# Two graph attention layers on one core: where a tile's own row joins its early sum

## The chip, the cores and the metric

The kernel runs on one core of a Trainium2 chip. The metric is the device time of one execution in microseconds (us), as the median of several runs. Beside it stands one profiled execution, from which every duration below is taken.

## The reference

Two layers of graph attention over 3327 nodes with 1024 features, with an adjacency matrix of zeros and ones (about 16 neighbours per node, each node its own neighbour too). Cut to what matters:

```python
def layer0(x, adj, W, a_src, a_dst):             # 8 heads of 128
    h = (x @ W).reshape(C, H, D)
    e = leaky_relu(alpha_src[:, :, None] + alpha_dst[:, None, :], 0.2)
    e = where(adj == 0, -inf, e)
    return softmax(e) @ h                        # per head

x = layernorm(x + layer0(x, adj, W0, a_src, a_dst))
x = layernorm(x + relu(layer1(x, adj, W1, a1, a2)))   # the same with one head
```

A node's result is a weighted mean of its neighbours' rows of h. The node's own row is one of them, with a weight of its own: per head the larger of two products of exponentials, times the diagonal of the adjacency matrix.

## The kernel before

Nodes are handled in 26 tiles of 128. The kernel has three stages.

**Stage one, tables and lists (0 to 604 us).** For each tile PE multiplies its x with the weight matrix in three column groups (`project`, L554), ACT copies each group out of PSUM (`keep`), and SP stores the row of h with its score factors to a table in HBM, `h0_d`. Two PSUM banks alternate for these groups. `flip` transposes x tiles on PE and ACT copies them (L204). Beside this, three Python generators are advanced a step at a time from inside `project`, by `pace`, four times in a column group, 12 times in a tile; the instruction order of every engine is this order, written out by hand.

- `counting`: a row of the adjacency matrix (loaded with a cast to bytes by POOL's queue into one of three masks `ad`) is counted by ACT (`words`, L354) and packed by DVE.
- `listing`: for each tile DVE takes the neighbours out of the packed words (`keys`, `columns`, L313, L315), ACT and DVE compute the place of each row's neighbours in the tile's list (`ways`, `places`, `spread`), PE sorts them into the list (`give`, L474, L467), ACT copies the list out (`take`, L486 to L493) and DVE turns it into indices (`sources`, L501 to L515). Before that, `ends` (L370) and `ends2` (L394) compute where each row's part of the list begins and ends: a small multiply by PE with a triangle of ones, a copy by ACT (L375, L395), and about ten small operations on POOL, once a tile each. `mvs` and `place_of` are their buffers, four of each.
- `sums_so_far` (from tile 13 on): the neighbours that lie in the first half of the table can be summed for 17 "early" tiles while the second half is still being computed. For each tile and each of two blocks, POOL issues four indirect gathers of `h0_d` rows (`fetch`, L672) into one of three buffers (`near`, `near`, `far`), DVE makes the weights (`marks`, `weights`, L689 to L693), and PE multiplies (`sums`, L702) into one PSUM tile of three banks. The generator yields nine times per early tile, so that it is spread over nine slots. At the end of a tile ACT copies the three parts to `z` (L742) and SP stores them to `half_d`.

```python
for n in range(3):
    nc.scalar.activation(by_head(z)[...], acc[:, n, :nh, :], AF.Copy)
nc.sync.dma_start(half_d[s], z)
```

**Stage two, layer 0 (604 to about 1190 us).** One tile after the other, late and early ones mixed, the first one late. Late tiles gather four blocks and a rest (17 indirect gathers), early ones two blocks and a rest (9), into five buffers. `prepare` loads the tile's own row of the table (L1077) and, for early tiles, the stored sum (L1080). DVE computes the own weights from the own row (`own`, L1086 to L1088), ACT scales the row head by head (`scale_own`, L1095), and PE adds it, and for early tiles the stored sum, to the sums in PSUM by a multiply with the identity (L1126). The gathered blocks are weighted by DVE (L1113) and summed by PE (L1139, L1131). `finish` divides, normalises and stores the row to a second table.

**Stage three, layer 1 (to 1844 us).** The same with one head from the second table, with a dense multiply after it (L1271).

Of the kernel before, what the change touches and what calls it, by code (L numbers as in the profile page):

```python
# [26 lines left out]
def kernel(  # L27
# [67 lines left out]
    XS = 256  # L95
    chunks = [(c, min(CT, NT - c)) for c in range(0, NT, CT)]
# [41 lines left out]
    def by_head(row):  # L138
        return row[:, :DW].rearrange("p (h d) -> p h d", h=H)

# [36 lines left out]
    class Phase:  # L177
# [84 lines left out]
        def edge_constants(self):  # L262
# [29 lines left out]
            self.mvs = [self.pool.tile([P, 3, NY], BF16, bufs=1, name=f"mvs{n}") for n in range(4)]  # L292
            for mv in self.mvs:
                nc.vector.memset(mv, 0.0)
                nc.vector.tensor_scalar(mv[:, 0, XN : XN + 1], nums, 1.0, None, op0=OP.add)
                nc.vector.tensor_scalar(mv[:, 0, NY - 1 :], part[:, 0, NB - 1 :], 1.0, None, op0=OP.add)
# [21 lines left out]

    class Edges:
# [6 lines left out]
        def __init__(self, ph, t):  # L326
            self.ph, self.t = ph, t
            self.d, self.end2 = cnt[:, t, :2], cnt[:, t, 2:3]

        def factors(self):  # L330

            mv = self.ph.mvs[self.t % 4][:, :, XR:XL]
            r = self.ph.sbuf("r0", [P, 2, H], 2)
            nc.scalar.activation(r[:, 0, :], sd0[:, self.t, 0, :], AF.Exp, scale=1 - SLOPE)
            nc.gpsimd.tensor_copy(mv[:, 0, :], r[:, 0, :])
            nc.gpsimd.tensor_tensor(r[:, 1, :], r[:, 0, :], mv[:, 0, :], OP.subtract)
            nc.gpsimd.tensor_copy(mv[:, 1, :], r[:, 1, :])
            nc.gpsimd.tensor_tensor(mv[:, 2, :], r[:, 1, :], mv[:, 1, :], OP.subtract)
# [8 lines left out]
        def words(self, ad, junk):  # L347

            sbuf = self.ph.sbuf
            for n in range(2):
                nc.scalar.activation(junk, ad[:, n * THR : (n + 1) * THR], AF.Copy, accum_out=self.d[:, n : n + 1])  # L354
            self.deg_b = sbuf("deg_b", [P, 2], 16, dt=BF16)
            nc.scalar.activation(self.deg_b, self.d, AF.Copy)
            w = ad.bitcast(I32)
            for n in range(3):
                m = WD >> n
                half = w[:, :m] if n == 1 else sbuf(f"wd{n}", [P, m], 16 if n == 2 else 1, dt=I32)  # L360
                nc.vector.scalar_tensor_tensor(
                    half, w[:, m:], 1 << n, w[:, :m], op0=OP.logical_shift_left, op1=OP.bitwise_or
                )
                w = half
            self.bytes = w.bitcast(U8)

        def ends(self, tri_b):

            op = self.ph.dd[:, self.t % 4 * 4 : self.t % 4 * 4 + 2]
            nc.tensor.matmul(op, tri_b, self.deg_b, start=True, stop=True)  # L370
            v = self.ph.sbuf("place_of", [P, 20], 4)
            end, off, low = (v[:, n : n + 2] for n in (0, 2, 4))
            self.mid, self.over = v[:, 6:8], v[:, 8:10]
            self.more, self.mid2, self.start, self.off2 = (v[:, n : n + 1] for n in range(10, 14))
            nc.scalar.activation(end, op, AF.Copy)  # L375
            self.more_b = self.ph.sbuf("more_b", [P, 1], 4, dt=BF16)
            nc.gpsimd.tensor_tensor(off, end, self.d, OP.subtract)
            nc.gpsimd.tensor_tensor(self.mid, off, end, OP.add)
            nc.gpsimd.tensor_scalar(low, off, float(HG2), None, op0=OP.max)
            nc.gpsimd.tensor_scalar(end, end, float(HG2), None, op0=OP.max)  # L380
            nc.gpsimd.tensor_tensor(self.over, end, low, OP.subtract)
            nc.gpsimd.tensor_tensor(self.more, self.over[:, :1], self.over[:, 1:], OP.add)
            nc.gpsimd.tensor_copy(self.more_b, self.more)
            nc.gpsimd.tensor_scalar(
                off[:, :1], off[:, :1], self.d[:, 1:], self.over[:, :1], op0=OP.subtract, op1=OP.subtract
            )
            mv = self.ph.mvs[self.t % 4][:, :, : XB + 1 : XB]
            nc.gpsimd.tensor_copy(mv[:, 0, :], off)
            nc.gpsimd.tensor_tensor(mv[:, 1, :], off, mv[:, 0, :], OP.subtract)

        def ends2(self, all_b):

            op = self.ph.dd[:, self.t % 4 * 4 + 2 : self.t % 4 * 4 + 3]
            nc.tensor.matmul(op, all_b, self.more_b, start=True, stop=True)  # L394
            nc.scalar.activation(self.end2, op, AF.Copy)  # L395
            nc.gpsimd.tensor_tensor(self.start, self.end2, self.more, OP.subtract)
            nc.gpsimd.tensor_tensor(self.mid2, self.start, self.end2, OP.add)
            nc.gpsimd.tensor_scalar(
                self.off2, self.start, self.d[:, 1:], self.over[:, 1:], op0=OP.subtract, op1=OP.add
            )  # L400
            mv = self.ph.mvs[self.t % 4][:, :, XE : XE + 1]
            nc.gpsimd.tensor_copy(mv[:, 0, :], self.off2)
            nc.gpsimd.tensor_tensor(mv[:, 1, :], self.off2, mv[:, 0, :], OP.subtract)
# [35 lines left out]
        def places(self):  # L439

            sbuf, ph, pack, away = self.ph.sbuf, self.ph, self.pack, self.away
            mv = self.mv = ph.mvs[self.t % 4]
# [75 lines left out]
    with ExitStack() as own, tc.manual_schedule():  # L518
# [10 lines left out]
        lists = [Edges(ph, t) for t in range(NT)]  # L529
# [6 lines left out]
        def load_mask(t):  # L536
            if t < NT:
                ads[t] = masks[t % 3]
                if t == NT - 1:
                    nc.vector.memset(ads[t].bitcast(I32), 0)  # L540
                    nc.vector.memset(ads[t][:, :1], 1.0)
                for r in pieces(t):
                    nc.gpsimd.dma_start(ads[t][r, :N], adj[at(t, r), :])
# [59 lines left out]
        def listing():  # L603

            for t in range(-1, NT):
                old, new = lists[t] if t >= 0 else None, lists[t + 1] if t + 1 < NT else None
                for s in range(4):
# [4 lines left out]
                    if s == 1 and 2 < t + 3 < NT:  # L612
                        need(t + 3)
                        lists[t + 3].ends(tri_b)
                    if s == 3 and 2 < t + 3 < NT:
                        lists[t + 3].ends2(all_b)
# [40 lines left out]
        def sums_so_far():  # L657

            acc = part.bank("L", [P, 3, HALF], "part")
            acc = acc[:, :, : 3 * DH1].rearrange("p n (h d) -> p n h d", h=3)  # L660
# [37 lines left out]
            def sums(acc, val, b, e, heads_):  # L698
                vals = val[:, :, :DW].rearrange("p g (h d) -> p g h d", h=H)
                for h in heads_:  # L700
                    for g in range(NG):
                        nc.tensor.matmul(  # L702
                            acc[g * GT : (g + 1) * GT, h // 3, h % 3, :], e[:, g, h, :], vals[:, g, h, :],
# [7 lines left out]

            res = [listed(0), listed(1)]
            for _ in range(3):
                yield
            for n in range(2):
# [3 lines left out]
                yield  # L719
            oh = marks(0)  # L720
            fetch(2)
            yield
            yield
            for s in range(EARLY):
                for b in range(HB):
                    n = s * HB + b
                    val = src[n % 3]
                    e = weights(val, b, res[0], oh)
                    yield
                    if n:  # L730
                        fetch(n + 2)
                    yield
                    sums(acc, val, b, e, range(H // 2))
                    yield
                    sums(acc, val, b, e, range(H // 2, H))
                    if b == 0:
                        yield
                        yield
                z = part.sbuf("z", [P, DW], 1)
                for n in range(3):  # L740
                    nh = HEADS[n + 1] - HEADS[n]
                    nc.scalar.activation(by_head(z)[:, HEADS[n] : HEADS[n + 1], :], acc[:, n, :nh, :], AF.Copy)  # L742
                nc.sync.dma_start(half_d[s], z)
                if s + 2 < EARLY:
                    res.append(listed(s + 2))
                res.pop(0)
                if s + 1 < EARLY:
                    oh = marks(s + 1)
# [21 lines left out]
        masks = [pool.tile([P, NP], U8, bufs=1, name=f"ad{n}") for n in range(3)]  # L770
# [56 lines left out]
        part.more_banks(own, "part", {"L": 1})  # L827
# [12 lines left out]
        ph.edge_constants()  # L840

# [15 lines left out]
        lists[0].ends(tri_b)  # L857
# [5 lines left out]
        lists[0].ends2(all_b)  # L863
        flip(3, 0)
        load_x(5)
        lists[1].ends(tri_b)
# [5 lines left out]
        lists[1].ends2(all_b)  # L872
# [3 lines left out]
        lists[2].ends(tri_b)  # L876
        project(3, 0)
        keep(3, 0)
        lists[2].ends2(all_b)
        for t in range(3, NT):  # L880
# [3 lines left out]
            if t == 12:  # L884
# [11 lines left out]
            if t == 16:  # L896
# [80 lines left out]
    def sparse(own):  # L977
# [82 lines left out]
        class Layer0:  # L1060
# [10 lines left out]
            def prepare(self):  # L1071
# [5 lines left out]
                nc.sync.dma_start(self.h, h0_d[self.t * P : (self.t + 1) * P, :HW0])  # L1077
                if self.t < EARLY:
                    self.half = sbuf("xT", [P, DW], 2, "half")
                    nc.sync.dma_start(self.half, half_d[self.t])  # L1080

            def own(self):

                t, h = self.t, self.h
                es = self.es = sbuf("es0", [P, H], 2)
# [4 lines left out]
            def scale_own(self):  # L1090

                h = self.h
                for n in range(H):
# [25 lines left out]
            def sums(self, b):  # L1119
# [3 lines left out]
                for n in self.banks.get(j, ()):  # L1123
                    for row in (self.h, self.half) if self.t < EARLY else (self.h,):
                        part = row[:, HEADS[n] * DH1 : HEADS[n + 1] * DH1]
                        nc.tensor.matmul(  # L1126
                            self.acc[n].rearrange("p h d -> p (h d)"), ident, part, start=False, stop=False
                        )
# [415 lines left out]
```

## Time and profile before

| | |
|---|---|
| median of 3 runs | 1784.67 us (1782.95 to 1788.36) |
| profiled execution | 1845.9 us |
| its span, first to last instruction | 1844.2 us |
| PE / DVE / POOL / ACT busy over the span | 88% / 62% / 59% / 28% |
| moved by DMA | 594.27 MB, mean 322 GB/s |
| mean granted TensorE clock | 0.943 |

A line of a window table gives the stretch, its length, then for PE, PEld (weight loads), DVE, ACT and POOL the busy time and the number of instructions, then the granted clock, the DMA share (busy share of the 16 DMA engines) and the GB/s moved. A line of the waits gives who waited for whom, the total, the number of times and the longest. The profile ends PE instructions by a model, so that a busy PE need not be PE at its peak[...].

### The profile page before, as it was taken

Reading aid. Unit: us, or ns where it says so; the run is one execution under the profiler, and the core shown is the slowest. Engines: PE = TensorE matmul, PEld = TensorE weight load, DVE = VectorE, ACT = ScalarE, POOL = GpSimd, SP = SyncE. Lnnn points to the kernel's source line nnn. Section 1 sums busy time; section 2 is a strip of 40 time slices with the busy share of each in tenths; the row PEclk is TensorE's granted clock in tenths of the full one; section 3 lists DMA queues with packets and bytes.
Section 4 is the critical chain, followed back from the end, with each engine's and each line's share of the span. In section 5 each row is a group of like instructions: output and inputs, shape, how many; then the busy total and the mean of one; then the engine's idle time right before and its main releaser. Section 6 shows DMA issues by size and latency. Waiting matters only on the chain.

```text
span 1844.2 us, 34940 instructions
## 1 busy us (share of the span) xinstructions
PE 1614.1 (88%) x12971; PEld 905.6 (49%) x12971; DVE 1142.9 (62%) x3132; ACT 524.0 (28%) x1506; POOL 1089.3 (59%) x1479
## 2 busy tenths in 40 slices
PE   8799989898998487877787876699999999999998
PEld 4566656565555354544554543244444444444443
DVE  5799997777765776877776685334444444344343
ACT  5678763332322122332332231011101111011110
POOL 4443356676655656566666656566666666666650
PEclk9899999999999788988988997799999999999999
DMA  7578977887879999999999999899999999999990
GB/s 188 96 145 151 178 189 264 285 289 277 284 255 356 363 371 396 408 399 396 399 395 386 391 396 383 298 369 390 379 379 375 379 386 379 393 386 386 365 350 34
DMA packets 189042, 594.27 MB, mean 322 GB/s; under 512 B 37069, under 2 KB 47079, under 8 KB 188864
## 3 DMA queue, kind: packets, MB, share of 16 engines
q0 software_dynamic: 131056, 460.61, 71.3%
q1 hardware_dynamic: 57650, 131.09, 19.2%
q8 instruction: 104, 1.70, 0.4%
q14 instruction: 74, 0.61, 0.1%
q10 hardware_dynamic: 158, 0.26, 0.0%
HBM read 592.01 MB, written 53.40 MB: 350 GB/s over the span
## 4 chain that ended last, share of the span: by engine, by line
PE 50%; issue 6%; DMA 6%; DVE 4%; ACT 0%; POOL 0%; SPq 0%; DVEq 0%; ACTq 0%; POOLq 0%
PE mm L1271 20%; PE acc L1239 14%; PE acc L1139 9%; PE acc L1126 4%; DMA own<-h_d 2%; PE acc L1131 2%; PE tr L201 1%; DMA near<-h_d,idx 1%; DVE pr L1003 1%; DVE e L1113 1%; DMA src<-h_d,idx 1%; DMA half<-half_d 1%; DVE y L1156 1%; DMA end<-y_d,idx 0%; DMA near<-y_d,idx 0%
## 5 line engine op out<-in xcount | busy, mean ns | idle before, releaser
L554 PE MATMUL mm<-wt,xT 128*128 128x384 f32 (+1 forms) x1248 | 413.5, 474 | 4.2 <-DMA wt<-in_L_gnn_W_dram 2.9
L1271 PE MATMUL mm<-wt,xT 128*128 128x512 f32 x832 | 388.0, 605 | 0.4 <-issue 0.3
L1037 POOL DMA_INDIRECT src<-y_d,idx x240 | 239.8, 999 | 119.0 <-issue 50.3
L554 PEld LDWEIGHTS mm<-wt,xT 128*128 128x128 f32 x1248 | 229.2, 195 | 124.3 <-issue 23.5
L1271 PEld LDWEIGHTS mm<-wt,xT 128*128 128x128 f32 x832 | 149.5, 189 | 199.7 <-issue 194.8
L1037 POOL DMA_INDIRECT src<-h_d,idx x168 | 178.6, 1063 | 112.7 <-PE acc L1139 40.1
L1274 DVE SCALAR_TENSOR_TENSOR o<-mm,y 128x512 f32<-128x512 f32 x52 | 36.0, 692 | 336.7 <-PE mm L1271 170.7
L1037 POOL DMA_INDIRECT near<-y_d,idx x176 | 176.5, 1003 | 104.6 <-PE acc L1239 48.5
L1139 PE MATMUL acc<-src,e 128*32 128x129 f32 x2688 | 139.8, 302 | 56.5 <-issue 41.3
L1139 PE MATMUL acc<-near,e 128*32 128x129 f32 x1792 | 103.8, 301 | 62.0 <-issue 38.2
L1037 POOL DMA_INDIRECT near<-h_d,idx x104 | 110.5, 1063 | 70.9 <-PE acc L1139 30.2
L1139 PEld LDWEIGHTS acc<-src,e 128*32 128x32 f32 x2688 | 91.9, 120 | 108.0 <-issue 81.6
L204 ACT ACTIVATE xT<-tr 128x512 f32<-128x512 f32 x104 | 63.4, 611 | 277.2 <-PE tr L201 216.9
L1113 DVE TENSOR_TENSOR e<-oh,way 128x1024 f32<-128x1024 f32 x96 | 117.2, 1221 | 23.8 <-PE acc L1139 7.5
L1239 PE MATMUL acc<-src,es 128*32 128x342 f32 (+1 forms) x1440 | 126.0, 455 | 2.0 <-issue 1.1
L1253 ACT ACTIVATE z<-y,ri 128x342 f32<-128x342 f32 (+1 forms) x78 | 39.5, 570 | 309.7 <-issue 123.5
L672 POOL DMA_INDIRECT near<-h_d,idx x96 | 104.4, 1087 | 38.7 <-issue 24.6
L1239 PE MATMUL acc<-near,es 128*32 128x342 f32 (+1 forms) x1056 | 98.0, 471 | 24.3 <-DVE es L1230 21.8
L1139 PEld LDWEIGHTS acc<-near,e 128*32 128x32 f32 x1792 | 64.0, 119 | 102.4 <-issue 84.1
L1095 ACT ACTIVATE own<-own,es 128x129 f32<-128x129 f32 x208 | 63.8, 390 | 72.9 <-DVE es L1088 38.1
L354 ACT ACTIVATE junk<-ad 128x1664 uint8<-128x1664 uint8 x52 | 82.9, 1594 | 3.4 <-POOL ad L343 1.7
L1126 PE MATMUL acc<-own,ident 128*128 128x387 f32 (+1 forms) x156 | 78.0, 586 | 6.0 <-ACT own L1095 4.0
(226 smaller groups left out, 2468.8 us busy)
## 6 DMA issues: line engine op xcount, KB each, us to landing
own<-h_d SPq DMA_DIRECT2D x26, 524.0 KB
y_d<-y SPq DMA_DIRECT2D x26, 514.0 KB
y<-y_d SPq DMA_DIRECT2D x26, 514.0 KB
h_d<-ht SPq DMA_DIRECT2D x25, 524.0 KB
x<-in_x_dram SPq DMA_DIRECT2D x25, 512.0 KB
y<-in_x_dram SPq DMA_DIRECT2D x25, 512.0 KB
out_dram<-o SPq DMA_DIRECT2D x25, 512.0 KB
ad<-in_adj_dram POOLq DMA_DIRECT2D x25, 415.9 KB
```

Source lines behind the costliest of these rows:

```text
L204: nc.scalar.activation(part, tr, AF.Copy)
L354: nc.scalar.activation(junk, ad[:, n * THR : (n + 1) * THR], AF.Copy, accum_out=self.d[:, n : n + 1])
L554: nc.tensor.matmul(acc, xT[t][:, k, :], wt[:, k, CUTS0[c] : CUTS0[c + 1]], start=k == 0, stop=k == KT - 1)
L672: nc.gpsimd.indirect_dma_start(out=src[n % 3][:, g, :], out_offset=None, in_=h0_d[:THR, :], in_offset=bass.IndirectOffsetOnAxis(ap=idx[:, ...
L1037: nc.gpsimd.indirect_dma_start(out=s[:, g, :w], out_offset=None, in_=table[:n, :], in_offset=bass.IndirectOffsetOnAxis(ap=idx[:, t, b * NG ...
L1095: nc.scalar.activation(h[:, d], h[:, d], AF.Copy, scale=self.es[:, n : n + 1])
L1113: nc.vector.tensor_tensor(e, oh.unsqueeze(2).to_broadcast([P, ng, H, wide]), wp.unsqueeze(3).to_broadcast([P, ng, H, wide]), OP.mult,)
L1126: nc.tensor.matmul(self.acc[n].rearrange("p h d -> p (h d)"), ident, part, start=False, stop=False)
L1139: nc.tensor.matmul(self.acc[h // 3][g * GT : (g + 1) * GT, h % 3, :], e[:, g, h, :], rowsof[:, g, h, :], start=j == 0 and h in HEADS, stop ...
L1239: nc.tensor.matmul(self.acc[c][to, :m], es[:, g, :], s[:, g, CUTS[c] : CUTS[c + 1]], start=b == 0, stop=b == EB,)
L1253: nc.scalar.activation(z[:, cut], self.res[:, cut], AF.Copy, scale=ri[:, 1:2])
L1271: nc.tensor.matmul(acc, xT[:, k, :], wt1[:, k, half], start=k == 0, stop=k == KT - 1)
```

## The change

1. **The own row joins the early sum.** `own_terms` computes the own weights of all early tiles from the scores in SBUF (`own_e`), in two goes. `own_row` loads a tile's own row from `h0_d` into one of two buffers, `scale` scales it on ACT, two heads at a time between the multiplies, and `settle` adds the three PSUM banks to it on DVE, in place. The result is stored to `half_d`. The buffers lie in the memory of the three masks, so all counts have to be made first (`need(NT - 1)`), and the order of the masks is turned by one. In stage two an early tile loads the stored row alone; `own` and `scale_own` do nothing for it, and PE adds one row.
2. **Single banks.** The early sums of a tile are three PSUM tiles of one bank each, in place of one tile of three banks.
3. **Order in the early sums.** The weights of the next block are made right after the multiplies of the one before, and the marks of the next tile before its last multiplies. `fetch` stands one slot earlier in a block.
4. **Ends for four tiles.** `ends` and `ends2` become a class `Ends` with `within` and `beyond`, which handle one tile for the first eight and then four at a time. `mvs` and `places` are rings of eight.
5. The diagonal of the adjacency matrix is loaded at tile 5 in place of 12 and converted at tile 11 in place of 16.

```diff
+            def own_terms(lo, hi):
+                mid = ph.sbuf("bits", [P, 8, KMAX], 1, dt=I32).rearrange("p a b -> p (a b)").bitcast(F32)
+                m, e = (hi - lo) * H, own_e[:, lo:hi, :]
+                mids = [mid[:, n * m : (n + 1) * m].rearrange("p (t h) -> p t h", h=H) for n in range(2)]
+                for n, scale in enumerate((1.0, SLOPE)):
+                    nc.scalar.activation(mids[n], sd0[:, lo:hi, 1, :], AF.Exp, scale=scale)
+                nc.scalar.activation(e, sd0[:, lo:hi, 0, :], AF.Exp, scale=1 - SLOPE)
+                nc.vector.tensor_tensor(e, e, mids[0], OP.mult)
+                nc.vector.tensor_tensor(e, e, mids[1], OP.max)
+                nc.vector.tensor_tensor(e, e, loop[:, lo:hi].unsqueeze(2).to_broadcast([P, hi - lo, H]), OP.mult)
+            def own_row(s):
+                if s < EARLY:
+                    nc.sync.dma_start(own_rows[s % 2], h0_d[s * P : (s + 1) * P, :DW])
+            def scale(s, heads_):
+                for h in heads_:
+                    d = by_head(own_rows[s % 2])[:, h, :]
+                    nc.scalar.activation(d, d, AF.Copy, scale=own_e[:, s, h : h + 1])
+            def settle(s, acc, n):
+                d = by_head(own_rows[s % 2])[:, HEADS[n] : HEADS[n + 1], :]
+                nc.vector.tensor_tensor(d, acc[n], d, OP.add)
...
             for s in range(EARLY):
+                acc = [part.bank("L", [P, HEADS[n + 1] - HEADS[n], DH1], "part") for n in range(3)]
                 for b in range(HB):
                     n = s * HB + b
-                    val = src[n % 3]
-                    e = weights(val, b, res[0], oh)
-                    yield
+                    val, last = src[n % 3], b == HB - 1
                     if n:
                         fetch(n + 2)
                     yield
+                    if last and s + 1 < EARLY:
+                        oh = marks(s + 1)
+                    yield
                     sums(acc, val, b, e, range(H // 2))
+                    scale(s, range(b * H // 2, b * H // 2 + 2))
                     yield
                     sums(acc, val, b, e, range(H // 2, H))
+                    if last:
+                        res.pop(0)
+                    if n + 1 < EARLY * HB:
+                        e = weights(src[(n + 1) % 3], (b + 1) % HB, res[0], oh)
+                    scale(s, range(b * H // 2 + 2, (b + 1) * H // 2))
                     if b == 0:
                         yield
                         yield
-                z = part.sbuf("z", [P, DW], 1)
+                if s == NTH - 3:
+                    own_terms(NTH, EARLY)
                 for n in range(3):
-                    nh = HEADS[n + 1] - HEADS[n]
-                    nc.scalar.activation(by_head(z)[:, HEADS[n] : HEADS[n + 1], :], acc[:, n, :nh, :], AF.Copy)
-                nc.sync.dma_start(half_d[s], z)
+                    settle(s, acc, n)
+                nc.sync.dma_start(half_d[s], own_rows[s % 2])
+                if s:
+                    own_row(s + 1)
                 if s + 2 < EARLY:
                     res.append(listed(s + 2))
-                res.pop(0)
-                if s + 1 < EARLY:
-                    oh = marks(s + 1)
                 yield
...
+        groups = {t: Ends(ph, t, 1) for t in range(RING)}
+        groups.update({t: Ends(ph, t, min(4, NT - t)) for t in range(RING, NT, 4)})
...
-                nc.sync.dma_start(self.h, h0_d[self.t * P : (self.t + 1) * P, :HW0])
                 if self.t < EARLY:
-                    self.half = sbuf("xT", [P, DW], 2, "half")
-                    nc.sync.dma_start(self.half, half_d[self.t])
+                    nc.sync.dma_start(self.h[:, :DW], half_d[self.t])
+                else:
+                    nc.sync.dma_start(self.h, h0_d[self.t * P : (self.t + 1) * P, :HW0])
...
-                for n in range(H):
+                for n in range(H if self.t >= EARLY else 0):
...
-                    for row in (self.h, self.half) if self.t < EARLY else (self.h,):
-                        part = row[:, HEADS[n] * DH1 : HEADS[n + 1] * DH1]
-                        nc.tensor.matmul(
-                            self.acc[n].rearrange("p h d -> p (h d)"), ident, part, start=False, stop=False
-                        )
+                    part = self.h[:, HEADS[n] * DH1 : HEADS[n + 1] * DH1]
+                    nc.tensor.matmul(self.acc[n].rearrange("p h d -> p (h d)"), ident, part, start=False, stop=False)
```

## The prediction

> **What bounds the kernel now.** I read the table of windows first, because the kernel has three stages and the page's shares average over them: tables of 26 tiles with the early sums beside them (0 to 604 us), layer 0 (604 to about 1190), layer 1 (to 1844). Columns: length, then busy us (and count) of PE, PEld, DVE, ACT, POOL, then granted clock, DMA share, GB/s.
>
> ```profile
> core 0: us, PE busy (x) PEld busy (x) DVE busy (x) ACT busy (x) POOL busy (x), PEclk, DMA share, GB/s
> ...
> 100.00:150.00 50.00, 50.00 (x227) 32.99 (x227) 47.28 (x135) 40.58 (x109) 19.76 (x71) 1.00 0.85 163
> ...
> 1300.00:1500.00 200.00, 199.13 (x1130) 86.98 (x1129) 85.07 (x256) 23.14 (x47) 133.29 (x134) 1.00 1.00 379
> ...
> 650.00:1000.00 350.00, 271.61 (x3510) 179.30 (x3508) 255.77 (x672) 103.70 (x268) 214.80 (x203) 0.90 1.01 393
> ...
> 250.00:604.00 354.00, 311.27 (x3126) 201.03 (x3125) 256.48 (x692) 113.14 (x432) 222.99 (x388) 0.95 0.81 283
> ```
>
> In layer 1 PE is busy 199.13 of 200 us: nothing but PE work counts there, and the change has none. In layer 0 PE has 78% and DVE 73%, but the DMA share is 1.01 at 393 GB/s: the bytes bound it. A check: a late tile moves 17 gathers of 128 rows of 4192 bytes (9.12 MB) and three rows of about 0.53 MB (own, x, result), 10.7 MB; an early one 9 gathers (4.83 MB) and four rows, 6.95 MB. 9 late and 17 early tiles make 214 MB, at 393 GB/s 546 us; the window 604 to 1150 is 546 us long. In the stretch of the early sums PE has 88% and DMA 0.81: PE bounds it, with gaps, and DMA has room. Next I read the waits of that stretch:
>
> ```profile
> DVE kq L501 <- ACT xs L488: 53.5, 12, 9.6
> ...
> ACT z L742 <- PE part L702: 33.4, 7, 11.9
> ...
> PE part L702 <- DVE e L693: 5.5, 3, 3.3
> ```
>
> The columns are total us, times, longest. DVE and ACT wait far longer for PE's results than PE waits for them. So both have slack, DVE's less (256 of 354 us busy). Then the chain in layer 0, start and length in us, where the own row stands:
>
> ```profile
> 719.42 10.22 DMA own<-h_d
> 729.66 0.17 DVE es L1086
> 729.86 0.18 DVE es L1087
> 730.04 0.29 ACTq L1095
> 730.38 2.45 ACT own L1095 x8
> ```
>
> The row is late by 10 us, DVE stands still for it with the next weights behind it (34.2 us in 11 waits from 640 to 1150), and eight ACT instructions follow before PE can add it.
>
> [...]
>
> **The change, part by part.**
>
> Layer 0, early tiles (17 of 26). Removed from SP's queue and the DMA engines: 17 loads own<-h_d of 128 x 1048 x 4 = 536,576 bytes, 9.12 MB. At 393 GB/s this is 23.2 us, on the bound. Removed beside it: 17 x 3 identity multiplies of the second row, 102 PE instructions (fp32 makes two of each); the chain has 8 of them in about 2.2 us, so 28 us of PE; 17 x 8 scalings at 390 ns = 53 us of ACT; 17 x 3 small DVE operations (166 + 167 + 276 ns) = 10 us; and DVE's stand before them (34.2 us x 17/26 = 22 us). I take nothing for these: they run beside transfers that already fill the time, though they make it likelier that the 23.2 us come out whole. If DMA no longer covers them, DVE at 73% is next, with 27% to spare. **Sum: -23.2**, bounds -31 (a third of DVE's stands was not covered) and -8 (the chain, not the bytes, sets the pace). The first tile of this stage is a late one, so the 5.23 us at its start stay.
>
> Early sums. 17 row loads of 128 x 1032 x 4 = 528,384 bytes, 8.98 MB, come onto SP's queue here: at layer 0's 2.57 us per MB some 23 us of DMA time in 354, share 0.81 to 0.88. No PE work is added. ACT gets 53 us of scaling and loses the 17 x (2 x 496 + 399) ns = 24 us of copies to z: 113 to 142 us of 354, covered by its waits for PE. [...]
>
> The new waits. (a) DVE's add waits for PE's last multiply of the tile; behind it stand the list steps and later weights. DVE was waiting for PE there anyway. (b) ACT's first scaling waits for the own row. z at 294.2 and at 597.4 us are 16 tiles apart: 19 us a tile, nine slots of 2.1 us each. The load is issued after the add and the half_d store, and the first scaling stands three slots on, 6.3 us. It lands after 1.55 (adds) + 2 x 0.32 (issues) + 5.2 = 7.4 us: ACT stands about 1.1 us, on 15 tiles (the first two rows are loaded well ahead). Behind it are PSUM copies for PE, which has the other of two banks and so a multiply group (about 5.5 us) in hand. I take 0.27 us of PE per tile, **+4**; bounds 0 and +40 (2.7 us each, if the row takes 10 us as in layer 0). (c) The first two own rows wait on SP for DVE's last counts, near 262 us; x loads and table stores behind them have a tile's time in hand: 0. (d) Gathers share with the new rows; DVE waits 8.3 us for them now. Half more, half covered: **+2**, bounds 0 and +10.
>
> What is taken off. Weights come right behind the previous multiplies: three or four slots ahead of PE in place of two. PE and PEld wait 5.5 and 7.5 us for e; a gain of up to 13, shared between the two queues: **-4**. The marks move with them, same cost. Single banks free each third of the sums as it is read; PE waits about 4 us for z in all, within that -4.
>
> Ends for four tiles. 26 pairs of steps become 8 + 5 = 13. PE loses 26 small multiplies of 165 ns, 4.3 us where PE bounds: **-4**, bounds -8 (half of the 7.8 us goes too that PE waits at L370 and L394) and 0. ACT loses 39 copies (0.2 us each), POOL some 200 instructions, 45 us, which ran beside other work. The four counts that a group needs are made by then: the counting runs ahead of the lists and ends at 262 us (L354), where the early sums begin, so no new wait. The diagonal's load and the last-mask condition move earlier: the small load (4.6 us of SP issue at 237.9) lies near 110 us instead, ahead of x loads with slack: 0, bound +3.
>
> **Sum**: -23.2 + 4 + 2 - 4 - 4 = -25.2 against the profiled 1845.9 us (span 1844.2 and 1.7 around it): 1820.7. The three runs have a median of 1784.67, 3.3% below the profiled one; their layer 1 can hardly be shorter, so layers before it are, and I scale the gain with the whole: 24.3 off, 1760 rounded to **1761**.
>
> **The rivals.**
> 1. *ACT's wait for the own row reaches PE (slower).* Place: the first scaling of each tile. Price: the row's 10 us in place of 5.2 makes ACT stand 6 us, more than a multiply group; 2.7 us of it pass to PE on 15 tiles, +40. It decides once PE loses over 1.7 us a tile (25/15). Then the sum is -29.2 + 40 = +10.8, scaled by 0.967 to 10.4, and with about 6 for gathers that come later too 1784.7 becomes 1801. For it: 10.22 us in the chain, and the load stands behind a store. Against: DMA is 0.81 busy there, not 1.01, and ACT has 60% of its time free.
> 2. *Layer 0 follows latencies, not bytes.* For it: the chain is mostly PE. Then the removed row gives 8: about 1776. Against: the byte count gives the stage's length within 1%.
> 3. *The early stretch gains too:* PE's 43 us of gaps there close by two fifths (17), as POOL no longer delays the factors (ACT waited 6.8 us in two cases). 1784.7 - 0.967 x (23 + 17) = 1746.
> 4. *It does not do what it says.* The built program's order shows 17 fewer row loads in layer 0, 17 more in the early stretch and 13 pairs of ends, so no chance is given to this.
>
> **How the numbers follow.** Forecast (1745 to 1775) 0.60; rival 1 0.20 (0.13 slower, 0.03 the same, 0.04 faster); rival 2 0.12 (0.08 faster, 0.04 the same); rival 3 0.08. With 0.02 of the forecast's mass given to slower: faster by over 0.3% 0.78, same 0.07, slower 0.15. 0.3%, 5.4 us, is about what a measurement of this kernel tells from no change. The range 1741 to 1789 joins a full gain in both stages (-45) to a row wait that eats the gain (+4).
>
> **What would show it.** Right: layer 0 some 23 us shorter with DMA still at 1.0 and 390 GB/s, no own scaling on early tiles; the early stretch within 8 us of 354, DMA share near 0.88; layer 1 unchanged. Wrong: ACT waits of over 2 us per tile for the own row with PE's copies late behind them; DVE adds that PE's list steps wait for; or a layer 0 with DMA share under 0.97 and little shorter.

## The result, and the profile after

| | before | after |
|---|---|---|
| median | 1783.92 us (1782.95 to 1788.36, 4 runs) | 1808.02 us (1803.06 to 1813.72, 4 runs) |
| ratio, 95% interval | | 1.0127 [1.0102, 1.0151] |
| profiled execution | 1845.9 us | 1803.15 us |

The change made the kernel 1.3% slower, 24 us, where 24 us of gain had been forecast.

Set side by side, the two profiled executions say the opposite, 1845.9 against 1803.15 us. That pair misleads: the profiled execution of before lay 3.4% above its own timed runs. So before was profiled again, in an execution of 1786.16 us. 

> The kernel before, profiled once more. Its earlier profiled execution took 1845.9 us, 3.4% above its timed runs, with layer 1 at 379 GB/s (25.3 us a tile), where the kernel after has 397 GB/s (24.3 us a tile). If that execution was slow in its DMA rate alone, this one takes about 1784, layer 1 near 621 us, layer 0 near 565 and the stage before layer 0 near 598, so that the change costs about 25 us before layer 0 and wins about 20 in it. Rival: layer 0 of the kernel before is already near 550 at this rate; then the removed loads won nothing there, and the loss before layer 0 is small too.

The window tables, first of the kernel after, then of the second execution of the kernel before (columns as in the prediction):

```profile
100.00:150.00 50.00, 45.49 (x203) 30.33 (x202) 37.33 (x106) 32.74 (x92) 16.57 (x72) 0.97 0.71 132
1300.00:1500.00 200.00, 200.00 (x1148) 86.44 (x1145) 88.08 (x264) 23.34 (x48) 140.59 (x139) 1.00 1.01 393
650.00:1000.00 350.00, 227.19 (x3597) 177.28 (x3601) 263.87 (x664) 76.73 (x170) 221.67 (x211) 0.82 1.00 387
250.00:604.00 354.00, 310.96 (x3169) 206.47 (x3167) 290.29 (x779) 140.18 (x528) 188.01 (x266) 0.96 0.86 306
```

```profile
100.00:150.00 50.00, 50.00 (x232) 33.03 (x231) 47.32 (x134) 40.90 (x110) 19.83 (x71) 1.00 0.85 163
1300.00:1500.00 200.00, 200.00 (x1168) 86.41 (x1167) 91.36 (x272) 24.14 (x50) 139.89 (x139) 1.00 1.02 395
```

First look at layer 1 (1300 to 1500). The change does not touch it. It moved 393 and 395 GB/s here, and 379 in the earlier profile of before, and its length below is 621.5 us in both profiles here and 643.7 in the earlier one. So the earlier execution moved its bytes more slowly, and only the second one may be held against after. Then look at 100 to 150 us: PE was busy 50.00 of 50 us and is now busy 45.49. Nothing of the own rows happens there yet.

Three markers in the traces divide the span: the first multiply of layer 0's sums, and the first and last dense multiply of layer 1.

| us | before, first profile | before, second | after |
|---|---|---|---|
| to the first layer 0 multiply | 608.2 | 582.4 | 623.5 |
| from there to layer 1's first dense multiply | 584.1 | 572.5 | 548.3 |
| layer 1 | 643.7 | 621.5 | 621.5 |

By these markers layer 0 gained 24.2 us. The stage before it lost 41.1, which is more than the 25 that were expected, as before's own stage is shorter than thought (582.4 in place of 598).

The markers flatter layer 0, though. In the second profile of before, POOL issues layer 0's first gather at 579.09 us, after 8.61 us of waiting for ACT's `grows`, and 3 gathers lie ahead of layer 0's first multiply. In after, the first is issued at 602.74 us without a wait, and 13 lie ahead of it. Ten gathers of 128 rows of 4192 bytes are 5.4 MB; at 393 GB/s that is some 14 us of transfers (an estimate) that have moved into the stage before. From layer 0's first gather to layer 1's first dense multiply the time fell by 6.7 us only, from 575.8 to 569.1.

The waits of the kernel after show where the stage before lost its time. First 40 to 250 us, then 250 to 630 us (total us, times, longest):

```profile
PE xp L338 <- ACT deg_b L336: 22.4, 10, 5.3
```

```profile
ACT ad L744 <- DMA ad<-h_d: 117.4, 15, 15.4
...
PE xp L488 <- ACT mvg L469: 11.4, 5, 4.1
...
PEld part L715 <- DVE ad L748: 10.3, 8, 4.7
...
PE part L715 <- DVE e L706: 7.1, 3, 3.7
...
PE part L715 <- DVE ad L748: 6.7, 5, 4.4
```

Two of these are new. PE stands 22.4 us for `deg_b`, ten times, where it stood once before (3.5 us in the second profile). And ACT stands 117.4 us in front of the own row, 7.8 us on average on 15 tiles.

The first wait, in the timeline of after (start, length, engine, line):

```profile
113.82 1.61 ACT L408 ACTIVATE junk<-ad 128x1664 uint8<-128x1664 uint8 x1
...
115.56 1.59 ACT L408 ACTIVATE junk<-ad 128x1664 uint8<-128x1664 uint8 x1
...
117.14 0.19 ACT L336 ACTIVATE deg_b<-cnt 128x2 bf16<-128x2 f32 x1
...
117.38 0.16 PE L338 MATMUL xp<-deg_b,tri_b 128*128 128x2 bf16 x1 [2.26 <-ACT deg_b L336]
117.39 2.23 PEld L568 LDWEIGHTS mm<-wt,xT 128*128 128x128 f32 x8 [2.34 <-issue]
117.41 2.83 PE L568 MATMUL mm<-wt,xT 128*128 128x384 f32 x8
```

ACT counts a later tile's mask for two times 1.6 us. Behind that stands the copy to `deg_b`, 0.19 us long, and PE's small multiply needs it. Behind the small multiply stand eight projection multiplies, for which the trace shows no wait of their own for ACT; they start 0.03 us after it.

The second wait, first on SP's queue, then on ACT:

```profile
419.50 0.32 SPq L795 DMA_DIRECT2D half_d<-ad  x1
419.91 0.38 SPq L739 DMA_DIRECT2D ad<-h_d  x1
```

```profile
413.83 1.27 ACT L744 ACTIVATE ad<-ad,own_e 128x129 f32<-128x129 f32 x4
418.07 0.49 ACT L586 ACTIVATE ht<-mm 128x384 f32<-128x384 f32 x1 [2.98 <-PE mm L568]
428.61 1.28 ACT L744 ACTIVATE ad<-ad,own_e 128x129 f32<-128x129 f32 x4 [10.05 <-DMA ad<-h_d]
429.80 0.58 ACT L500 ACTIVATE xs<-xp 128x512 f32<-128x512 f32 x1
```

ACT is ready for the next tile's scaling at 418.56 us (428.61 less 10.05). The row's load is issued only at 419.91, because it stands on SP's queue behind the store of the sum before, and that waits for DVE's adds. The row is there 8.70 us later. Behind the scaling stand copies out of PSUM; the first of them (`xs`, L500) starts only at 429.80. In this tile PE still had other work: it was busy 24.00 of 24 us from 408 to 432. Five tiles on it did not:

```profile
529.73 1.28 ACT L744 ACTIVATE ad<-ad,own_e 128x129 f32<-128x129 f32 x4 [10.63 <-DMA ad<-h_d]
530.91 1.26 ACT L469 ACTIVATE mvg<-mvs,own_g 128x129 bf16<-128x129 bf16 x4
```

PE's sort (`xp`, L488) needs that `mvg`; it starts at 532.23 us, and PE had stood idle for 4.08 us. The last row costs most directly. ACT waits 15.38 us for it, to 605.47 us, with the early sums finished at 600.9. Its sum and store stand ahead of layer 0, and PE is idle for 22.57 us between the two stages, against 12.96 before.

### The profile page after: what moved, and what is told of

Its sections match the earlier page's. It is cut to its first block, busy times and chain, and to the rows that moved or that the text cites. A ratio compares the mean times of both kernels' runs of the same rounds, so it can differ in the third digit from the quotient of the medians.

```text
span 1801.4 us, 34408 instructions
## 1 busy us (share of the span) xinstructions
PE 1489.1 (83%) x12843; PEld 870.4 (48%) x12843; DVE 1157.3 (64%) x3129; ACT 497.9 (28%) x1422; POOL 1038.4 (58%) x1310
## 4 chain that ended last, share of the span: by engine, by line
PE 39%; DMA 15%; DVE 8%; issue 3%; POOL 0%; ACT 0%; DVEq 0%; SPq 0%; ACTq 0%; POOLq 0%
PE mm L1326 21%; PE acc L1294 13%; DMA src<-h_d,idx 7%; DMA near<-h_d,idx 3%; PE acc L1194 3%; DVE e L1171 3%; DVE y L1211 1%; PE tr L204 1%; DMA src<-y_d,idx 1%; DMA near<-y_d,idx 1%; DMA end<-h_d,idx 1%; DVE pr L1059 1%; DVE st L225 1%; DMA av<-in_L_gnn_a_dram 1%; PE acc L1186 1%
## 5 line engine op out<-in xcount | busy, mean ns | idle before, releaser
L1093 POOL DMA_INDIRECT src<-y_d,idx x240 | 243.9, 1016 | 94.3 <-issue 29.4
L1194 PE MATMUL acc<-src,e 128*32 128x129 f32 x2688 | 117.5, 346 | 80.2 <-DVE e L1171 80.2
L1194 PEld LDWEIGHTS acc<-src,e 128*32 128x32 f32 x2688 | 98.9, 141 | 104.0 <-DVE e L1171 88.5
L1194 PE MATMUL acc<-near,e 128*32 128x129 f32 x1792 | 71.2, 323 | 67.8 <-DVE e L1171 45.2
L1294 PE MATMUL acc<-src,es 128*32 128x342 f32 (+1 forms) x1440 | 115.9, 454 | 0.4 <-DVE es L1285 0.4
L1294 PE MATMUL acc<-near,es 128*32 128x342 f32 (+1 forms) x1056 | 89.7, 475 | 26.0 <-DVE es L1285 26.0
L1194 PEld LDWEIGHTS acc<-near,e 128*32 128x32 f32 x1792 | 60.3, 131 | 80.1 <-DVE e L1171 49.7
L1183 PE MATMUL acc<-own,ident 128*128 128x387 f32 (+1 forms) x156 | 67.1, 533 | 25.4 <-ACT own L1153 24.4
L744 ACT ACTIVATE ad<-ad,own_e 128x129 f32<-128x129 f32 x136 | 45.0, 404 | 117.4 <-DMA ad<-h_d 117.4
```

Source lines behind the costliest of these rows:

```text
L744: nc.scalar.activation(d, d, AF.Copy, scale=own_e[:, s, h : h + 1])
L1093: nc.gpsimd.indirect_dma_start(out=s[:, g, :w], out_offset=None, in_=table[:n, :], in_offset=bass.IndirectOffsetOnAxis(ap=idx[:, t, b * NG ...
L1183: nc.tensor.matmul(self.acc[n].rearrange("p h d -> p (h d)"), ident, part, start=False, stop=False)
L1194: nc.tensor.matmul(self.acc[h // 3][g * GT : (g + 1) * GT, h % 3, :], e[:, g, h, :], rowsof[:, g, h, :], start=j == 0 and h in HEADS, stop ...
L1294: nc.tensor.matmul(self.acc[c][to, :m], es[:, g, :], s[:, g, CUTS[c] : CUTS[c + 1]], start=b == 0, stop=b == EB,)
```

## The experiments

**One cause at a time, then both.** All three were timed in one set, with the kernel before at a median of 1783.13 us (28 runs); after is from the earlier set, where before took 1783.92.

The copy back in the count:

```diff
-            deg_b = sbuf("deg_b", [P, 4, 2], 2, dt=BF16)[:, :n]     # in within()
-            nc.scalar.activation(deg_b, d, AF.Copy)
+            deg_b = self.ph.degs[:, self.t : self.t + n]
...
+            nc.scalar.activation(self.ph.degs[:, self.t, :], self.d, AF.Copy)   # in words()
```

> The kernel after, with the bf16 copy of the counts made by ACT right after the counts, as before, in place of right before the small multiply that reads it. Theory 1 (the late copy makes PE stand behind ACT's 1.6 us junk counts, twice a tile): the stretch from 50 to 250 us gets some 8 to 12 us shorter, the wait of PE xp for ACT deg_b falls from 22.4 us in 10 to under 6, and the time is 1790 to 1798. Theory 2 (the own rows' wait alone costs the time): same as after within 3 us, 1800 to 1808.

The row issued half a tile sooner:

```diff
+                    if b == 0 and s:
+                        own_row(s + 1)
                     sums(acc, val, b, e, range(H // 2, H))
...
                 nc.sync.dma_start(half_d[s], own_rows[s % 2])
-                if s:
-                    own_row(s + 1)
```

> The kernel after, with the load of the next own row issued in the middle of a tile of early sums (once the store that used its buffer is behind it by half a tile) in place of at its end. Theory 2 (ACT's wait for the own row, 7.8 us on each of 15 tiles, reaches PE over its PSUM copies): ACT's wait of 117 us falls under 15, the stretch from 250 us to the end of the sums gets 10 to 20 us shorter, time 1788 to 1798. Theory 1 (only the late copy matters): ACT's wait falls as well, the time stays within 4 us of after, 1800 to 1808.

> Both edits. If the layer 0 gain of some 20 us is real and the two waits are all that ate it: 1770 to 1782, below the kernel before. If the rows that were moved forward cost DMA time where they are now, or the gain in layer 0 is not real: 1785 to 1800.

| | median us (runs) | ratio to before, 95% | stage before layer 0 | layer 0 | layer 1 |
|---|---|---|---|---|---|
| after | 1808.02 (4) | 1.0127 [1.0102, 1.0151] | 623.5 | 548.3 | 621.5 |
| copy in the count | 1785.36 (20) | 1.0005 [0.9994, 1.0017] | 608.0 | 548.5 | 621.5 |
| row sooner | 1775.62 (9) | 0.9954 [0.9940, 0.9969] | 596.1 | 548.2 | 621.5 |
| both | 1757.78 (4) | 0.9855 [0.9832, 0.9878] | 577.3 | 547.5 | 622.1 |

Each edit alone takes off more than was expected of it, 22.7 and 32.4 us. Both together take off 50.2, and 1757.78 us lies below either range that had been expected. The stage lengths of the profiles give less: 15.5, 27.4 and 46.2. Two of after's four runs lie at 1803 and two at 1813, and its profile is one of the former. So the copy cost 15 to 23 us and the row 27 to 32. Neither theory that names one cause alone stands. All the difference lies in the stage before layer 0, as the table shows. With the copy in the count, the wait of 40 to 250 us is again the one of before:

```profile
PE xp L338 <- ACT degs L409: 3.5, 1, 3.5
```

and PE is busy 50.00 us again from 100 to 150. With both edits, ACT's wait for the row in 250 to 630 us has fallen from 117.4 us to

```profile
ACT ad L745 <- DMA ad<-h_d: 6.1, 3, 4.6
```

PE's idle time from 250 us to layer 0's first multiply is 61.3 us with the copy in the count alone and 37.2 with both edits, so ACT's wait did reach PE. Some 6 us of this lie between the two stages (22.3 and 16.1 us idle).

The kernel with both edits beats before and after, by 25 and 50 us.

**The late copy in the kernel before.** Does the place of the copy cost the time by itself, without groups of four and own rows?

```diff
-            self.deg_b = sbuf("deg_b", [P, 2], 16, dt=BF16)            # in words()
-            nc.scalar.activation(self.deg_b, self.d, AF.Copy)
...
+            self.deg_b = self.ph.sbuf("deg_b", [P, 2], 16, dt=BF16)    # in ends()
+            nc.scalar.activation(self.deg_b, self.d, AF.Copy)
             nc.tensor.matmul(op, tri_b, self.deg_b, start=True, stop=True)
```

> The kernel before with one edit: the bf16 copy of the counts is made right before the small multiply that reads it, as in the kernel after; ends stay single, own rows stay in layer 0. If the place of the copy alone costs the time: PE waits for ACT deg_b over 20 us between 40 and 250 us in place of 3.5, time 1800 to 1812. If it costs only together with the groups of four or the own rows: within 5 us of the kernel before, 1778 to 1788.

This and the following runs were made on another chip of the kind, where the kernel before takes 1844 us, so only ratios and kernels of this chip are compared. Its traces show layer 1 at 378 to 380 GB/s, as in the first profile of before, where the traces of the first chip show 391 to 395. Measured: 1862.53 us (5 runs) against 1843.97 (16 runs), ratio 1.0126 [1.0074, 1.0178] (the ratios are not quotients of the two medians, and differ a little from them). Waits of 40 to 250 us:

```profile
PE xp L370 <- ACT deg_b L368: 25.1, 12, 5.3
```

The stage before layer 0 took 630.3 us, against 608.2 in the first profile of before: 22 us more. This profile is the slowest of the five runs (1878.66 us; the others 1861.59 to 1863.06), so the 19 us of the medians are the safer figure. The place of one 0.2 us copy thus costs some 15 to 23 us in either kernel.

**Was it bytes in layer 0?** To the kernel with both edits, a load of the own row comes back in layer 0, and nothing else:

```diff
                     nc.sync.dma_start(self.h[:, :DW], half_d[self.t])
+                    nc.sync.dma_start(sbuf("xT", [P, DW], 2, "half"), h0_d[self.t * P : (self.t + 1) * P, :DW])
```

> The kernel with both edits, and in layer 0 each early tile again loads its own row of 528 KB from the layer's table on SP's queue, into a buffer of its own that nothing reads; no arithmetic comes back. If the bytes set layer 0's length (the prediction's step, 23 us for 17 rows): layer 0 gets 20 to 24 us longer (547.5 to about 570), time 1776 to 1784. If the chain of latencies, the identity multiplies or the scalings that fell away gave the gain: under 8 us, time up to 1766.

With the unread rows it took 1824.53 us (13 runs). The kernel with both edits was not timed beside it; its variant with the first bank sooner, which the last set below puts within 3 us of it, was, with 1807.00 (4 runs). Difference: 17.5 us. Held against the 1813.95 us of the kernel with both edits itself in the later set, it is 10.6. Layer 0 took 581.0 us; in the five profiles on this chip without the unread rows, 563.0 to 573.1. So bytes alone carry some 11 to 18 us of layer 0's gain, below the expected 20 to 24 and above the rival's 8. The rest of the 24.2 is of about the size of what the earlier gathers take ahead of the marker (some 14 us by the estimate above for ten of them; with both edits nine more than before lie ahead of it). What the multiplies (102 at L1126 of before on the one row of the early tiles, two for each of the program's 51), scalings (390 ns each at L1095) and small steps that fell away are worth, and what the difference of the chips does, no run tells.

**Groups of four, and the first bank sooner.** Two edits to the kernel with both edits:

```diff
-        groups = {t: Ends(ph, t, 1) for t in range(RING)}
-        groups.update({t: Ends(ph, t, min(4, NT - t)) for t in range(RING, NT, 4)})
+        groups = {t: Ends(ph, t, 1) for t in range(NT)}
```

> The kernel with both edits, with the ends of rows taken for one tile at a time throughout (26 pairs of steps) in place of 13. The prediction's step gives groups of four 4 us: time 1759 to 1766. Rival: the group asks PE for four tiles' counts at once and the copy of it back lands later for all; then single ends are as fast or faster, 1750 to 1758.

```diff
                     if last:
                         res.pop(0)
+                        settle(s, acc, 0)
                     if n + 1 < EARLY * HB:
                         e = weights(src[(n + 1) % 3], (b + 1) % HB, res[0], oh)
...
-                for n in range(3):
+                for n in range(1, 3):
                     settle(s, acc, n)
```

> The kernel with both edits, with DVE's add for the first bank issued ahead of the next weights (its three heads are done in the first half of the last block) in place of behind them. In the trace with both edits PE and PEld wait 12.2 and 17.0 us for DVE's adds at the next tile's first multiply. If that wait sets PE's pace: it falls by half or more, time 1745 to 1754. If PE then waits for the weights that come 0.56 us later, or the gaps are covered by the projection's multiplies: 1755 to 1761, no change.

They gave 1814.87 us (4 runs; ratio to before 0.9890 [0.9823, 0.9958]) and 1807.00 (4 runs; 0.9838 [0.9783, 0.9892]), on the second chip, without the kernel with both edits beside them. One more set has all three:

> The kernel with both edits once more, beside the next two on one chip: the chips differ (the kernel before took 1783 in one set of runs and 1844 in another), so single ends and the sooner add have no base of their own yet. On a chip where before takes about 1783: 1754 to 1760; where it takes 1844: 0.9855 of it, about 1817. If the two repairs are worth less where DMA is slower, the ratio is above 0.99.

> The sooner add for the first bank, beside the kernel with both edits on one chip. If DVE's adds set the pace at the next tile's first multiply: 3 to 10 us below it. If the gaps were covered: within 3 us.

> Single ends, beside the kernel with both edits on one chip. The prediction's step: 2 to 8 us above it. Rival (the group's later copy costs as much as it saves): within 2 us or below.

| | median us (range, runs) | ratio to before, 95% |
|---|---|---|
| both edits | 1813.95 (1810.20 to 1816.99, 6) | 0.9846 [0.9812, 0.9880] |
| and first bank sooner | 1811.54 (1804.69 to 1821.53, 6) | 0.9838 [0.9796, 0.9880] |
| and single ends | 1821.60 (1817.79 to 1823.65, 5) | 0.9883 [0.9845, 0.9922] |

The ratio of both edits is the same on the two chips within its interval (0.9855 and 0.9846). Single ends cost 7.6 us, with no overlap of the single times in this set, though the two intervals to before overlap. The rival is not supported. The sooner add changes the time by nothing that shows. Yet the wait that it aimed at is gone from the list. Waits of 250 to 620 us, kernel with both edits, on this chip, then with the sooner add:

```profile
PEld part L716 <- issue: 29.3, 55, 1.3
...
PEld part L716 <- DVE ad L749: 10.3, 8, 4.0
PE part L716 <- DVE ad L749: 6.8, 4, 3.7
```

```profile
PEld part L716 <- issue: 42.7, 69, 4.0
```

The rows for DVE's adds are gone, and PEld's time that no release explains grew from 29.3 to 42.7 us, and that of PE's sums from 10.5 to 17.6. So the idle time stayed and only its entry changed. What holds PE there is not shown.

## Why the prediction was wrong

**What failed first: "The four counts that a group needs are made by then ... so no new wait" (Ends for four tiles).** The counts were made by then; the bf16 copy of them was not. The diff takes it out of `words` and puts it one line ahead of the small multiply in `within`. The step counted the instructions of the group (fewer of them) and asked whether their data exist, but not where the first of them stands on its engine. In the trace of after the copy starts at 117.14 us, right behind the second count (115.56 us, 1.59 us long) and the read of its sum (117.05 us). For the groups themselves the step was within its bounds (-4, down to -8, where single ends cost 7.6 us on the other chip). What it left out, as "no new wait", measured +15 to +23 (copy back in the count) and +19 to +22 (copy late in the kernel before). It also fell into the stretch of 40 to 250 us, where PE had been busy 50.00 of the 50 us from 100 to 150, so that it had no idle time there to make up a wait.

**What failed second: the own row's wait, priced +4 with bounds 0 and +40.** The mechanism was named, the size was wrong in two of its terms. "The first scaling stands three slots on, 6.3 us": over the 15 tiles, ACT reached the scaling a median of 0.14 us after the row's issue, and before the issue on seven of them. Slots order the work; here they did not hold ACT back, and it had 60% of its time free, which the prediction read as safety. "+ 5.2": issue to start was 8.2 us in the median (4.7 to 10.4), nearer to the 10.22 us of the chain in layer 0 (DMA share 1.00 in that time) than to the 5.23 us of the row at 605 us (0.96), which stands at the end of this paragraph. "1.55 (adds)" was near: a tile's three adds take 1.53 us in after (two of 554 ns and one of 420). 8.2 - 0.14 is about the 7.8 us that the wait shows, in place of 1.1. That is more than the 5.5 us that the prediction gave PE in hand, so a part passes. It cost 32.4 us by the row sooner alone, or 27.6 (1785.36 - 1757.78) on top of the first repair: 1.8 to 2.2 us a tile in the mean. The loss is not even: the wait at 418 us cost PE nothing, the one at 519 us 4 us, and the last row some 6 us where the stage ends and nothing covers it, a place that the prediction did not price. Rival 1 had the wait's mechanism, its threshold (1.7 us a tile) and nearly its price (2.7). That its total of 1801 lies near the measured 1808 is partly luck, as it had nothing of the late copy. Its other part, 6 us for gathers that come later, is not supported: with both edits DVE's `w` waits 12.1 us for gathers in 250 to 630 us, and 19.4 (15.5 and 3.9) in the second profile of before. The row at 605 us, in the chain of before:

```profile
605.18 5.23 DMA own<-h_d
```

**What held.** *Layer 1 unchanged*: 621.5 and 621.5. *Gathers, +2*: that wait did not grow (6.5 us in after, 19.4 in the second profile of before). *ACT in the 354 us from 250 to 604*: 142 us busy had been worked out, 140 were measured. DVE was busy 290 us there, against 256 and 278 in the two profiles of before (the second has layer 0's first 22 us in that window); the 51 adds took 24.9 in all.

**What held in its number, partly by luck.** *Layer 0, -23.2*: the markers give -24.2, with DMA share 1.0 and the own rows and scalings gone from the early tiles. But bytes put back were worth 11 to 18 us, not 23.2, and part of the 24.2 are gathers that now run ahead of the marker, which the prediction did not have. Rival 2 gave 8 us to the layer, less than the bytes alone. *The sum without the two waits*: 24.3 had been forecast, and 25.3 is what both edits gain (1783.13 to 1757.78), but its terms were sized otherwise.

**What held only in part.** *Weights earlier, -4*: PE and PEld waited 13.0 and 16.2 us for `e` in the second profile of before, and 6.4 and 8.3 with both edits. But "single banks free each third as it is read, within that -4" left out that DVE's adds (0.55 and 0.42 us each in after) stand behind the next weights: 12.2 and 17.0 us of waits for them came in place. Making the first of these adds sooner gained nothing that shows.

**A reading that was wrong without consequence: "nothing but PE work counts there" of layer 1.** PE's busy share was 99.6%, but DMA was at 1.00 too. On the two chips the same multiplies took 621.5 and about 644 us, with the granted clock at 1.00 and the DMA share at 1.0 on both. PE's clock was not lower, so the transfers are what is likely to count there; no run changes them in layer 1 alone. PE's busy time did not tell the two apart: 199.13 of 200 us with 1130 instructions in the first profile of before, 200.00 with 1168 in the second. From the same reading came "their layer 1 can hardly be shorter" for the timed runs; in the second profile it is 22.2 us shorter. Scaling the gain with the whole kept this from mattering.

## What to carry to other kernels

When a step is moved, look for the first instruction on its new way that another engine waits for, and ask what stands ahead of it on its own queue: a copy of 0.2 us cost about 20 us by standing behind two long counts, while PE's other work stood behind the multiply that needed it. An engine with much idle time may be at its next wait before the load is even issued: ACT, with 60% of its time free, was so on seven of 15 tiles, and stood 117.4 us in all with its later work behind it. So time a load from the moment when that engine gets there, not from slots in the program, and with what loads take in that stretch (here 8.2 us in the median, not 5.23). Hold two profiles against each other only after a stage that the change does not touch agrees in both, and when a stage seems shorter, ask whether its transfers have only started earlier.

## What the runs showed of the hardware

Two chips gave times for the same kernel that differ by 3.4% (medians of 1783.13 and 1843.97 us), and layer 1 ran at 391 to 395 and 378 to 380 GB/s at a DMA share of 1.0 on both. A share of 1.0 thus did not tell here how much was moved. In after, from 250 to 604 us at a DMA share of 0.86, a row of 528,384 bytes on SP's queue took 4.7 to 10.4 us, 8.2 in the median, from issue to the start of the reader that waited for it.
